# Conditions' and values' bias products moved to the gap in front of the second layer, scale and shift in four operations, bounds of the reciprocals behind the norm

## The chip, the cores and the metric

The kernel runs on one core of a Trainium2 chip. Such a core has a matrix engine (TensorE, PE in the profile; PEld is its weight load, which overlaps), three engines for element-wise work (VectorE or DVE, ScalarE or ACT, GpSimd or POOL) and SyncE (SP), which here does nothing but issue transfers. Each engine takes its instructions in a fixed order from a queue of its own and waits on semaphores for the others. The metric is the time of one execution on the device in microseconds (us); of several executions the median is given.

## The reference

32 sequences of 128 tokens with 512 features go through two layers. `cond` is one vector of 512 for each sequence. Cut to what matters:

```python
# layer 0: attention with 16 heads of 64, then 8 experts that choose their tokens
shift = silu(cond) @ W_ada.T + b_ada
h = ln(x) + shift
q, k, v = split(h @ Wqkv.T);  q, k = ln(q), ln(k)
x = x + softmax(q k^T / sqrt(64)) v @ Wout.T
gate = softmax(tok @ Wgate.T);  vals, idx = top_k(gate.T, 512)
y = gelu(ln(tok[idx]) @ fc1[e].T + b1) @ fc2[e].T + b2
tok = tok.at[idx].add(y * vals)

# layer 1: adaptive norm, attention with 16 heads of 32, adaptive norm, MLP of 2048
def adaln(x, w, b):
    scale, shift = split(cond @ w.T + b)
    return layernorm(x) * (1 + scale) + shift
n = adaln(x, w_adaln1, b_adaln1)
q, k, v = n @ wq.T + bq, n @ wk.T + bk, n @ wv.T + bv
x = x + softmax(q k^T / sqrt(32)) v @ wo.T + bo
h = gelu(adaln(x, w_adaln2, b_adaln2) @ w1.T + b1)
x = x + h @ w2.T + b2
```

Two small products matter for the change. The conditions' product is `cond @ w.T` for both adaptive norms of layer 1: 32 rows by 1024 columns each. The values' bias `bv` is not added to v: since the weights of a softmax add up to one, it can be added behind the attention, as `bv @ wo.T`, to the bias `bo`. That is the values' bias product.

## The kernel before

All work of the fast kernel is first declared as operations: engine, planned duration, buffers that are read and written, a priority number (smaller is earlier) and a job. A list scheduler in the same file (`Sched`) then plans them in time and writes out, for each engine, one fixed order of instructions. Buffers are taken from pools while it plans: 11 weight slots of 1 MB (128 × 4 × 512 float32), 52 row slots of 128 × 512, and 8 banks of PSUM, the matrix engine's accumulators. So a changed priority, or an operation more or less, can change the order of other work and the slots that it takes.

The stages are these:

- **Layer 0** takes two sequences at a time: 16 pairs, whose jobs overlap. Matrix products are cut into quarters and done with seven products in place of eight, with sums of weights made beforehand. `weight_sums` (L1260 to L1274) makes some of these sums on DVE. In the same stage, at low priority, sums of the weights of layer 1 are prepared and stored in memory (the loop over `at_w`, L2067 to L2083).
- **Routing** finds each expert's 512 tokens while PE does the late projections of the last sequences. Then each of the **8 experts** gathers its token rows with indirect transfers (POOL), normalises them, does two products (`u` L1854 and `d` L1918), and adds its output to the rows of `acc` in memory with an indirect transfer that adds (L1950). The last expert does its second product in two halves.
- **Layer 1** takes two sequences at a time: 16 groups. Group 0 can't begin before the last expert's addition has landed in memory. It loads its two sequences (`x2`, L2158), computes mean and variance (L317, L318) and the reciprocal root in steps of DVE on 128 × 2 elements (L299 to L307), normalises (`a_0n`, L2124), transposes on PE (`a_0t`, L1084), and applies scale and shift in the evictions of the transposed tile (`nT`, L2134 on DVE and L2136 on ACT, which read `ss`). The products `qk` (L2193), scores, exponentials and sums follow; `inv` (L1119) is the reciprocal of the softmax's sums, and `oT` (L2312) the normalised output of the heads. Sums of `oT` (`noa`, `nob`, L1108) are operands for the out-projection `o` (L2239); `seven_T` writes the order of its seven products, and of those of `v`. Bias and residual are added to `x3` (L2277 on), whose norm feeds the MLP, `m` (L2359) and `n` (L2420).

What the change touches, as it is before:

- The conditions' products, L1218 to L1240: in the job of the first pair four weight loads of 1 MB (`wad`, L1093) are issued on SP; two times 8 matmuls `pad` (L1229; each is two records of the profile) leave 64 × 512 results, which are copied into one row tile `pads` (ACT L1099 or DVE L1100). In the routing stage four transposes turn them (`ptd`), and 16 operations of DVE (L1238) add the bias, and one for the scale, into `ss1` and `ss2`. `weight_sums` names `pads` among what it reads.
- The values' bias product: in the preparation of `wo`, four copies spread `bv` over 128 columns (`bvb`, L2071), `bo` is loaded (L2073), 8 matmuls `pb` (L2078) take them, DVE adds (L2081), and the result is stored to memory (`bod`, L2015). In layer 1 it is loaded into `bo_t` (L2110).
- The gathers of the experts but the first have a priority 1000 ahead of their expert.
- The two loads of group 0's `x2` are on SP's queue.
- `hi_t` (L2314, POOL) and `lo_t` (L2316, DVE) keep the running sum and the running minimum of the reciprocals; their final values (L2470 to L2478) tell whether the fast kernel's way of taking a softmax without a maximum was safe. Both come directly behind `oT` in priority.

Of the kernel before, what the change touches and what calls it, by code (L numbers as in the profile page):

```python
# [1006 lines left out]
def fast_kernel(ctx: ExitStack, tc: tile.TileContext, x, condT, mask, cols, w_ada, wqkv, wout, wout_p, wout_o, wgate,  # L1007
# [209 lines left out]

    pads, ptd = row("pads"), bank("ptd", (P, 4, P))  # L1218
    RJ = NB // 2
    RP = NB * 100 + 200  # L1220
    for n, (s_, pr, job) in enumerate(((w_adaln1, 140, 1), (w_adaln2, 145, 1))):
        wad = [load_w(s_, 0, j * 512, f"wad_{n}_{j}", 140 + 5 * n, 1, 20.0) for j in range(2)]
        pad = bank(f"pad_{n}")

        def adaln(n=n, wad=wad, pad=pad):
            for k in range(DC):
                for j in range(2):
                    g = 2 * n + j
                    nc.tensor.matmul(pad.t[32 * g : 32 * g + 32, :], cT[:, k, :], wad[j].t[:, k, :],  # L1229
                                     start=(k == 0), stop=(k == DC - 1))  # L1230
        sch.op(PE, mm_us(D, 4), adaln, w=[pad], r=wad, prio=pr, job=job)
        copy([(pads, n)], [pad], lambda n=n: pads.t[64 * n : 64 * n + 64, :], lambda n=n, pad=pad: pad.t[64 * n : 64 * n + 64, :],
             D, pr, job)
    sch.op(PE, 4 * TR, lambda: transpose4(flat(ptd), pads.t), w=[ptd], r=[pads], prio=RP + 900, job=RJ)
    for n, (ss, ssb, nm) in enumerate(((ss1, ss1_b, "b_adaln1"), (ss2, ss2_b, "b_adaln2"))):
        for h in range(2):
            for c in range(4):
                sch.op(DVE, 0.2, lambda ss=ss, nm=nm, n=n, h=h, c=c: nc.vector.tensor_scalar(  # L1238
                    ss[:, 4 * h + c, :], ptd.t[:, c, (2 * n + h) * 32 : (2 * n + h) * 32 + NB], col(nm, 4 * h + c),
                    1.0 - h, ALU.add, ALU.add), w=[(ssb, 4 * h + c)], r=[ptd], prio=RP + 900, job=RJ)  # L1240
# [20 lines left out]
    def weight_sums():  # L1261
        for k in range(2):
            for i, a_, b_, r_ in ((1, lambda k=k: wV(1, 2, k), lambda k=k: wV(1, 1, k), [wqkv_b[4], wqkv_b[5]]),
                                  (2, lambda k=k: wV(2, 2, k), lambda k=k: tv[1][k].t, [wqkv_b[5], tv[1][k]]),
                                  (3, lambda k=k: wV(2, 2, k), lambda k=k: wV(1, 2, k), [wqkv_b[5]]),
                                  (4, lambda k=k: wV(2, 1, k), lambda k=k: tv[2][k].t, [wqkv_b[4], tv[2][k]])):
                o_ = (lambda k=k: wV(1, 2, k)) if i == 3 else (lambda i=i, k=k: tv[i][k].t)
                tt(o_, a_, b_, ALU.subtract, D, [wqkv_b[5] if i == 3 else tv[i][k]], r_ + [pads], 154, 1, DVE, False)
        for n in range(2):
            for i, a_, b_, r_ in ((1, lambda n=n: wB(1, 2, n), lambda n=n: wB(1, 1, n), [wqkv_b[n + 2], wqkv_b[n]]),  # L1270
                                  (2, lambda n=n: wB(2, 2, n), lambda n=n: wT(1, n), [wqkv_b[n + 2], (t12[n], 0)]),
                                  (3, lambda n=n: wB(2, 2, n), lambda n=n: wB(1, 2, n), [wqkv_b[n + 2]]),
                                  (4, lambda n=n: wB(2, 1, n), lambda n=n: wT(2, n), [wqkv_b[n], (t12[n], 1)])):
                tt(lambda i=i, n=n: wT(i, n), a_, b_, ALU.subtract, 2 * D, [wTb(i, n)], r_ + [pads], 155, 1, DVE, False)  # L1274
# [466 lines left out]
    def expert(e, after):  # L1741
# [13 lines left out]
        for h in range(NH):  # L1755
            sch.op(POOL, 1.2, lambda h=h: nc.gpsimd.indirect_dma_start(
                out=xg[h].t, out_offset=None, in_=tok[:, :],
                in_offset=bass.IndirectOffsetOnAxis(ap=idx[:, e, h : h + 1], axis=0)),
                w=[xg[h]], r=[tok_b, (idx_b, e)], lat=2.5, prio=pe_ - 1000 if e else pe_, job=job)
# [255 lines left out]
    bod = dram.tile([P, D], F32, name="bod")  # L2015
    bod_b = stands(bod)
# [10 lines left out]
    sch.op(POOL, 0.5, lambda: nc.gpsimd.memset(lo_b.t, 1.0), w=[lo_b], r=[up_done], prio=LB - 800, job=LJ)  # L2027

# [35 lines left out]
    for m, (n, s_) in enumerate(at_w):  # L2064
        pr, job = 200 * (10 + m) + 195, 10 + m
        q = quarters(s_, f"{n}q_", lambda i, j: (QD * (i - 1), QD * (j - 1)), pr, job)
        if n == "o":  # L2067

            bvb, bos, pb0 = row("bvb", (P, DC, P)), row("bos"), bank("pb0")
            for c in range(DC):  # L2070
                sch.op(DVE, 0.3, lambda c=c: nc.vector.tensor_copy(bvb.t[:, c, :], col("bv", c).to_broadcast([P, P])),  # L2071
                       w=[(bvb, c)], prio=pr - 2, job=job)
            sch.op(SP, 0.06, lambda: nc.sync.dma_start(bos.t, bo.partition_broadcast(P)), w=[bos], lat=4.0, prio=pr - 2, job=job)  # L2073

            def bias0(q=q, bvb=bvb, pb0=pb0):
                for l in (1, 2):
                    for c in range(DC):
                        nc.tensor.matmul(pb0.t[:, (l - 1) * QD : l * QD], bvb.t[:, c, :], q[1 + c // 2, l].t[:, c % 2, :],  # L2078
                                         start=(c == 0), stop=(c == DC - 1))
            sch.op(PE, mm_us(D, DC), bias0, w=[pb0], r=[bvb, *q.values()], prio=pr - 1, job=job)  # L2080
            sch.op(DVE, dve_us(D), lambda: nc.vector.tensor_tensor(bos.t, bos.t, pb0.t, ALU.add), w=[bos], r=[bos, pb0],  # L2081
                   prio=pr - 1, job=job)
            store(bod[:, :], bos, bod_b, None, pr, job)  # L2083
        A = lambda i, j, q=q: q[j, i]
        sa, sb, sc_ = (row(f"{n}s{z}_", (P, 2, QD)) for z in "124")
        for o_, a_, b_, op_ in ((sa, A(2, 1), A(2, 2), ALU.add), (sb, sa, A(1, 1), ALU.subtract),
                                (A(2, 1), A(1, 1), A(2, 1), ALU.subtract), (sc_, A(1, 2), sb, ALU.subtract)):
            tt(lambda o_=o_: o_.t, lambda a_=a_: a_.t, lambda b_=b_: b_.t, op_, D, [o_], [a_, b_], pr, job, DVE, False)
        for z, b_ in enumerate((sa, sb, A(2, 1), sc_)):
            store(s4d[m, z], b_, s4d_b, (m, z + 1), pr, job)  # L2090
# [19 lines left out]
    sch.op(SP, 0.06, lambda: nc.sync.dma_start(bo_b.t, bod[:, :]), w=[bo_b], r=[up_done, bod_b], lat=4.0, prio=LB - 800, job=LJ)  # L2110
# [41 lines left out]
    def group(g):  # L2152
# [4 lines left out]
        for i in range(GB):  # L2157
            sch.op(SP, 0.06, lambda i=i: nc.sync.dma_start(x2[i].t, acc[(b0 + i) * S : (b0 + i + 1) * S, :]),  # L2158
# [70 lines left out]
        def seven_T(n, Bn, rB, Tv, Tn, pr, first, comb, out2):  # L2229
# [16 lines left out]
            out2(1, 1, U[1], ps[2])  # L2246
            prod(6, "s2", lambda: Tv(2), [Tn[2]])
# [10 lines left out]
            prod(3, "s4", lambda: Bn(2, 2), rB(2, 2))  # L2258
# [15 lines left out]
        for i in range(GB):  # L2274
# [27 lines left out]
            def outs(po=po, pe=pe, i=i):  # L2302
                for t in range(4):
# [11 lines left out]
                   w=[hi_b], r=[inv], prio=pa + 20, job=job)  # L2315
            sch.op(DVE, dve_us(D), lambda inv=inv: nc.vector.tensor_tensor(lo_b.t, lo_b.t, flat(inv), ALU.min),  # L2316
                   w=[lo_b], r=[inv], prio=pa + 8, job=job)
# [249 lines left out]
```

## Time and profile before

| | us |
|---|---|
| median of 3 runs | 3264.16 (3264.08 to 3264.27) |
| the profiled execution | 3265.81 |
| its span, first to last instruction | 3264.1 |
| layer 0 | 0 to about 1000 |
| routing, late projections, first gather | about 1000 to 1108 |
| experts | 1108 to 1917.3 |
| gap in front of layer 1 | 1917.3 to 1930.6 |
| layer 1 | 1930.6 to the end |

The span in 40 equal slices; each digit is the busy share of a slice in tenths, and PEclk the clock granted to PE in tenths of full speed. A slice is 81.6 us.

```profile
PE   8999999999999899999999989999999999999999
DVE  7877876787777888666676547666666666666665
ACT  3333332343441122211222213333333333333332
POOL 0011111000023467766676510000000000000000
PEclk9999999999999899999999999999999999999999
```

PE is at nine tenths or more in all slices but three: the first, the routing's, and the one that holds the gap. The profile can miss a few per cent of the matmul records. The clock stands at 0.993 on average.

### The profile page before, as it was taken

Reading aid. Unit: us, or ns where it says so; the run is one execution under the profiler, and the core shown is the slowest. Engines: PE = TensorE matmul, PEld = TensorE weight load, DVE = VectorE, ACT = ScalarE, POOL = GpSimd, SP = SyncE. Lnnn points to the kernel's source line nnn. Section 1 sums busy time; section 2 is a strip of 40 time slices with the busy share of each in tenths; the row PEclk is TensorE's granted clock in tenths of the full one; section 3 lists DMA queues with packets and bytes.
Section 4 is the critical chain, followed back from the end, with each engine's and each line's share of the span. In section 5 each row is a group of like instructions: output and inputs, shape, how many; then the busy total and the mean of one; then the engine's idle time right before and its main releaser. Section 6 shows DMA issues by size and latency. Waiting matters only on the chain.

```text
span 3264.1 us, 55856 instructions
## 1 busy us (share of the span) xinstructions
PE 3204.9 (98%) x21802; PEld 2563.0 (79%) x21802; DVE 2265.9 (69%) x4849; ACT 962.0 (29%) x2307; POOL 709.8 (22%) x561
## 2 busy tenths in 40 slices
PE   8999999999999899999999989999999999999999
PEld 4565566555558688888888878999999999999998
DVE  7877876787777888666676547666666666666665
ACT  3333332343441122211222213333333333333332
POOL 0011111000023467766676510000000000000000
PEclk9999999999999899999999999999999999999999
DMA  5122211321125423433333542333333333333343
GB/s 210 52 66 84 67 55 56 113 82 65 46 91 196 160 86 102 117 110 106 102 110 94 152 142 92 105 101 101 102 100 100 102 98 99 101 100 101 104 136 105
DMA packets 247138, 335.65 MB, mean 103 GB/s; under 512 B 22098, under 2 KB 156498, under 8 KB 246354
## 3 DMA queue, kind: packets, MB, share of 16 engines
q1 hardware_dynamic: 239698, 315.09, 29.4%
q0 software_dynamic: 7168, 16.91, 2.8%
q8 instruction: 174, 2.85, 0.4%
q14 instruction: 98, 0.80, 0.1%
HBM read 277.01 MB, written 54.92 MB: 102 GB/s over the span
## 4 chain that ended last, share of the span: by engine, by line
PE 60%; DVE 2%; issue 1%; ACT 1%; DMA 1%; SPq 0%; DVEq 0%; ACTq 0%
PE m L2359 12%; PE d L1918 12%; PE u L1854 11%; PE n L2420 10%; PE qk L2193 6%; PE v L2239 3%; PE o L2239 2%; PE sc L2289 1%; PE ps L2300 1%; PE po L2306 1%; DVE lo_t L2316 1%; DVE inv L1119 0%; DVE noa L1108 0%; PE tpg L1084 0%; DVE inv_1t L1117 0%
## 5 line engine op out<-in xcount | busy, mean ns | idle before, releaser
L2314 POOL TENSOR_TENSOR hi_t<-hi_t,inv 128x512 f32<-128x512 f32 x32 | 40.8, 1276 | 1229.9 <-DVE inv L1119 1229.9
L2370 ACT ACTIVATE m<-m,prm 128x128 f32<-128x128 f32 x512 | 162.0, 390 | 230.4 <-DVE m L2364 226.3
L1918 PE MATMUL d<-fc,h 128*128 128x256 f32 x992 | 219.0, 380 | 0.6 <-DVE v L1859 0.6
L1918 PEld LDWEIGHTS d<-fc,h 128*128 128x128 f32 x992 | 187.9, 190 | 26.1 <-DVE v L1859 0.8
L1865 ACT ACTIVATE h<-h,prm 128x256 f32<-128x256 f32 x256 | 114.9, 500 | 258.0 <-DVE h L1859 250.6
L1854 PE MATMUL u<-gT,fc 128*128 128x256 f32 x768 | 179.0, 383 | 1.0 <-ACT gT L1824 1.0
L1854 PEld LDWEIGHTS u<-gT,fc 128*128 128x128 f32 x768 | 147.7, 193 | 21.9 <-ACT gT L1824 1.4
L2364 DVE TENSOR_TENSOR m<-mu,m 128x512 f32<-128x512 f32 x128 | 87.9, 687 | 110.2 <-PE m L2359 107.9
L1300 ACT ACTIVATE sq<-qk 128x512 f32<-128x512 f32 x128 | 80.8, 632 | 215.5 <-DVE qk L1338 205.9
L2364 DVE TENSOR_TENSOR mu<-mu,m 128x512 f32<-128x512 f32 x96 | 65.9, 686 | 88.1 <-PE m L2359 88.1
L2359 PE MATMUL m<-n2a,w_s 128*128 128x128 f32 x1024 | 124.8, 275 | 0.0
L2420 PE MATMUL n<-w_t,m 128*128 128x256 f32 x512 | 122.8, 379 | 0.0
L1854 PE MATMUL u<-tg,s 128*128 128x256 f32 x512 | 120.9, 379 | 0.9 <-DVE tg L1108 0.9
L2359 PE MATMUL m<-n2T,w 128*128 128x128 f32 x1024 | 120.0, 275 | 0.2 <-ACT n2T L2136 0.2
L2359 PEld LDWEIGHTS m<-n2a,w_s 128*128 128x128 f32 x1024 | 119.5, 192 | 0.0
L2359 PEld LDWEIGHTS m<-n2T,w 128*128 128x128 f32 x1024 | 118.3, 192 | 1.4 <-ACT n2T L2136 0.4
L1859 DVE TENSOR_TENSOR h<-v,u 128x512 f32<-128x512 f32 x128 | 86.3, 681 | 47.7 <-PE u L1854 46.1
L2420 PE MATMUL n<-w_t,ms 128*128 128x256 f32 x512 | 117.8, 382 | 0.0
L2420 PE MATMUL n<-w,m 128*128 128x256 f32 x512 | 114.7, 382 | 0.0
L1334 PE MATMUL q<-wqkv,hsb 128*128 128x512 f32 x240 | 113.8, 597 | 0.1
L1334 PE MATMUL q<-wqkv,hT 128*128 128x512 f32 x240 | 113.9, 606 | 0.0
L1918 PE MATMUL d<-t,hs 128*128 128x256 f32 x512 | 113.4, 379 | 0.0
(1155 smaller groups left out, 7537.9 us busy)
## 6 DMA issues: line engine op xcount, KB each, us to landing
w_t<-t2d SPq DMA_DIRECT2D x256, 256.0 KB, 3.1
w<-in_w_dram SPq DMA_DIRECT2D x192, 256.0 KB, 4.1
fc<-in_fc_dram SPq DMA_DIRECT2D x64, 512.0 KB, 4.4
fc<-in_fc_dram SPq DMA_DIRECT2D x32, 1024.0 KB, 5.3
x<-in_x_dram SPq DMA_DIRECT2D x32, 256.0 KB, 3.1
xT<-in_xT_dram SPq DMA_DIRECT2D x32, 256.0 KB, 2.7
otd<-oT SPq DMA_DIRECT2D x32, 256.0 KB, 2.1
ol<-otd SPq DMA_DIRECT2D x32, 256.0 KB, 4.1
```

The costliest lines, as they stand in the source:

```text
L1300: sch.op(ACT, act_us(D), lambda: nc.scalar.activation(sq.t, qk[i][j].t, AF.Square), w=[sq], r=[qk[i][j]], prio=pr, job=job)
L1334: nc.tensor.matmul(ps[m].t, lhs()[:, k, :], rhs[0](k), start=(k == 0), stop=(k == 1))
L1854: nc.tensor.matmul(ps[n].t[:, t, :], lhs()[:, k, t * P : (t + 1) * P], rhs.t[:, k, :], start=(k == 0), stop=(k == 1))
L1859: sch.op(DVE, dve_us(D), lambda: nc.vector.tensor_tensor(o_.t, a_.t, ps[n].t, ALU.add), w=[o_], r=[a_, ps[n]], prio=pr, job=job)
L1865: sch.op(ACT, act_us(HQ, 1), lambda t=t, c=c: nc.scalar.activation(o_.t[:, t, :], o_.t[:, t, :], AF.Gelu_apprx_tanh, bias=col("b1s", e * 1 ...
L1918: nc.tensor.matmul(ps[n].t[:, j, :], lhs[m].t[:, k, t * P : (t + 1) * P], rhs.t[:, 2 * m + k, :], start=(m == 0 and k == 0), stop=(m == NM ...
L2193: nc.tensor.matmul(ps[m].t[:, z, u, :], w_()[:, k, u * P : (u + 1) * P], rhs()[:, k, :], start=(k == 0), stop=(k == 1))
L2239: nc.tensor.matmul(ps[m].t, lhs()[:, k, :], w_()[:, k, :], start=(k == 0), stop=(k == 1))
L2359: nc.tensor.matmul(ps[n].t[:, u, :], l1w[what].t[:, k, (NQ * q + u) * P : (NQ * q + u + 1) * P], rhs()[:, k, :], start=(k == 0), stop=(k = ...
L2364: sch.op(DVE, dve_us(D), lambda: nc.vector.tensor_tensor(o_.t, a_.t, ps[n].t, ALU.add), w=[o_, *more], r=[a_, ps[n]], prio=pq_, job=job)
L2370: sch.op(ACT, act_us(S, 1), lambda u=u, c=c: nc.scalar.activation(o_.t[:, u, :], o_.t[:, u, :], AF.Gelu, bias=col("b1", c), scale=1.0), w= ...
L2420: nc.tensor.matmul(ps[n].t, Ah[lhs][c // NQ].t[:, c % NQ, :], b_.t[:, k, :], start=(c == 0), stop=(c == 7))
```

## The change

- The conditions' products with their loads and copies, the transposes, and the scale and shift move to the job of layer 1's group 0. The loads may start when the last expert's first product is done (`up_done`). The priorities put the products at LB − 824 and LB − 823, the transposes and the scale and shift at LB − 822, where LB is the priority from which layer 1 counts.
- Scale and shift are 4 operations of DVE in place of 16: each takes 128 × 4 × 32 elements and a broadcast bias.
- `weight_sums` no longer names `pads`.
- The gathers of the experts from the third on have their own expert's priority.
- The values' bias product moves to group 0's job as well. It takes the out-projection's quarters that layer 1 loads in any case, and a fourth quarter (`wo21`) loaded for it. `bo` is loaded directly into `bo_t`, and DVE adds the product there; the memory tile `bod` and its store and reload are gone.
- Group 0's two loads of `x2` are issued by ACT.
- `seven_T` writes its third product behind the second, in place of last.
- `hi_t` and `lo_t` get priorities behind the work of their group's second norm.

```diff
-    pads, ptd = row("pads"), bank("ptd", (P, 4, P))
...
-    for n, (s_, pr, job) in enumerate(((w_adaln1, 140, 1), (w_adaln2, 145, 1))):
-        wad = [load_w(s_, 0, j * 512, f"wad_{n}_{j}", 140 + 5 * n, 1, 20.0) for j in range(2)]
...
-    sch.op(PE, 4 * TR, lambda: transpose4(flat(ptd), pads.t), w=[ptd], r=[pads], prio=RP + 900, job=RJ)
...
-            for c in range(4):
-                sch.op(DVE, 0.2, lambda ss=ss, nm=nm, n=n, h=h, c=c: nc.vector.tensor_scalar(
-                    ss[:, 4 * h + c, :], ptd.t[:, c, (2 * n + h) * 32 : (2 * n + h) * 32 + NB], col(nm, 4 * h + c),
-                    1.0 - h, ALU.add, ALU.add), w=[(ssb, 4 * h + c)], r=[ptd], prio=RP + 900, job=RJ)
...
-                tt(o_, a_, b_, ALU.subtract, D, [wqkv_b[5] if i == 3 else tv[i][k]], r_ + [pads], 154, 1, DVE, False)
+                tt(o_, a_, b_, ALU.subtract, D, [wqkv_b[5] if i == 3 else tv[i][k]], r_, 154, 1, DVE, False)
...
-                w=[xg[h]], r=[tok_b, (idx_b, e)], lat=2.5, prio=pe_ - 1000 if e else pe_, job=job)
+                w=[xg[h]], r=[tok_b, (idx_b, e)], lat=2.5, prio=pe_ - 1000 if e == 1 else pe_, job=job)
...
+    pads, ptd = row("pads"), bank("ptd", (P, 4, P))
+    for n, (s_, pr, job) in enumerate(((w_adaln1, LB - 824, LJ), (w_adaln2, LB - 823, LJ))):
+        wad = [load_w(s_, 0, j * 512, f"wad_{n}_{j}", LB - 985 + n, LJ, r=[up_done]) for j in range(2)]
+        pad = bank(f"pad_{n}")
+
+        def adaln(n=n, wad=wad, pad=pad):
+            for k in range(DC):
+                for j in range(2):
+                    g = 2 * n + j
+                    nc.tensor.matmul(pad.t[32 * g : 32 * g + 32, :], cT[:, k, :], wad[j].t[:, k, :],
+                                     start=(k == 0), stop=(k == DC - 1))
+        sch.op(PE, mm_us(D, 4), adaln, w=[pad], r=wad, prio=pr, job=job)
...
+    sch.op(PE, 4 * TR, lambda: transpose4(flat(ptd), pads.t), w=[ptd], r=[pads], prio=LB - 822, job=LJ)
+    for n, (ss, ssb, nm) in enumerate(((ss1, ss1_b, "b_adaln1"), (ss2, ss2_b, "b_adaln2"))):
+        for h in range(2):
+            at = COL[nm] + 4 * h
+            sch.op(DVE, 0.3, lambda ss=ss, n=n, h=h, at=at: nc.vector.scalar_tensor_tensor(
+                ss[:, 4 * h : 4 * h + 4, :], ptd.t[:, :, (2 * n + h) * 32 : (2 * n + h) * 32 + NB], 1.0 - h,
+                bcast(prm[:, at : at + 4], NB), ALU.add, ALU.add), w=[(ssb, h)], r=[ptd], prio=LB - 822, job=LJ)
...
-            bvb, bos, pb0 = row("bvb", (P, DC, P)), row("bos"), bank("pb0")
...
-            sch.op(PE, mm_us(D, DC), bias0, w=[pb0], r=[bvb, *q.values()], prio=pr - 1, job=job)
...
-            store(bod[:, :], bos, bod_b, None, pr, job)
...
-    sch.op(SP, 0.06, lambda: nc.sync.dma_start(bo_b.t, bod[:, :]), w=[bo_b], r=[up_done, bod_b], lat=4.0, prio=LB - 800, job=LJ)
+    sch.op(SP, 0.06, lambda: nc.sync.dma_start(bo_b.t, bo.partition_broadcast(P)), w=[bo_b], r=[up_done], lat=4.0, prio=LB - 800, job=LJ)
+
+    bvb, pb0, wo21 = row("bvb", (P, DC, P)), bank("pb0"), row("wo21", (P, 2, QD))
+    for c in range(DC):
+        sch.op(DVE, 0.3, lambda c=c: nc.vector.tensor_copy(bvb.t[:, c, :], col("bv", c).to_broadcast([P, P])),
+               w=[(bvb, c)], r=[up_done], prio=LB - 890, job=LJ)
+    load_at("o21", lambda: wo21.t, wo21, wo[:QD, QD:].rearrange("(k p) n -> p k n", p=P), [up_done], LB - 945, spare=8)
+
+    def bias0():
+        for i in (1, 2):
+            for c in range(DC):
+                nc.tensor.matmul(pb0.t[:, (i - 1) * QD : i * QD], bvb.t[:, c, :], l1w[f"o{i}{1 + c // 2}"][0]()[:, c % 2, :],
+                                 start=(c == 0), stop=(c == DC - 1))
+    sch.op(PE, mm_us(D, DC), bias0, w=[pb0], r=[bvb] + [l1w[f"o{i}{j}"][1] for i in (1, 2) for j in (1, 2)], prio=LB - 821, job=LJ)
+    sch.op(DVE, dve_us(D), lambda: nc.vector.tensor_tensor(bo_b.t, bo_b.t, pb0.t, ALU.add), w=[bo_b], r=[bo_b, pb0],
+           prio=LB - 815, job=LJ)
...
-            sch.op(SP, 0.06, lambda i=i: nc.sync.dma_start(x2[i].t, acc[(b0 + i) * S : (b0 + i + 1) * S, :]),
+            sch.op(*((SP, 0.06) if g else (ACT, 0.1)), lambda i=i: (nc.sync if g else nc.scalar).dma_start(
+                x2[i].t, acc[(b0 + i) * S : (b0 + i + 1) * S, :]),
...
             out2(1, 1, U[1], ps[2])
+            prod(3, "s4", lambda: Bn(2, 2), rB(2, 2))
             prod(6, "s2", lambda: Tv(2), [Tn[2]])
...
-            prod(3, "s4", lambda: Bn(2, 2), rB(2, 2))
             out2(1, 2, U[4], ps[3])
...
-                   w=[hi_b], r=[inv], prio=pa + 20, job=job)
+                   w=[hi_b], r=[inv], prio=pr + 197, job=job)
...
-                   w=[lo_b], r=[inv], prio=pa + 8, job=job)
+                   w=[lo_b], r=[inv], prio=pr + 196, job=job)
```

## The prediction

> **What bounds the kernel now.** I read the busy shares first, then what TensorE waited for, then the busy time by stretches, then the chain of waits and the timeline round the three places that the change touches.
>
> ```profile
> PE 3204.9 (98%) x21802; PEld 2563.0 (79%) x21802; DVE 2265.9 (69%) x4849; ACT 962.0 (29%) x2307; POOL 709.8 (22%) x561
> ```
>
> TensorE (PE) is busy for all but 59 us, so two things can shorten the run: less matmul time in a stretch where PE is full, or less idle PE time. Its waits, largest first (columns: total us, times, longest us):
>
> ```profile
> PE tpg L1084 <- DVE xng L1812: 14.3, 3, 12.8
> PE a_0t L1084 <- DVE a_0n L2124: 13.3, 1, 13.3
> PE tpx L1084 <- DVE xn L1399: 12.6, 3, 10.1
> PE o L2239 <- DVE noa L1108: 4.2, 13, 0.3
> ```
>
> The second is the gap in front of layer 1: the last expert's output is scattered to memory, read back and normalised, with nothing for PE to do. The fourth is a small wait in nearly every group of layer 1. Three stretches follow (stretch, length, busy time of PE, PEld, DVE, ACT, POOL, granted clock, DMA share, GB/s): layer 0, the gap, and the first products behind it.
>
> ```profile
> 600.00:1000.00 400.00, 400.00 (x3006) 226.24 (x3003) 302.57 (x697) 169.13 (x442) 41.45 (x35) 1.00 0.23 78
> 1918.00:1930.00 12.00, 0.00 (x0) 0.00 (x0) 3.54 (x15) 0.00 (x0) 1.55 (x1) 0.68 0.66 174
> 1933.00:1936.00 3.00, 3.00 (x16) 3.00 (x16) 2.24 (x7) 0.97 (x3) 0.00 (x0) 0.50 1.02 406
> ```
>
> Layer 0 has no PE slack (140 to 600 us lacks only 2.4 us); the gap has 12 us of it; and the clock is granted at 0.50 for some 6 us behind the gap.
>
> **Products taken out of layer 0.** The conditions' products (pad, 32 matmul records) and the values' bias products (pb, 16 records) leave layer 0 and the weight preparation. What they hold there:
>
> ```profile
> 104.08 3.63 PE L1229 MATMUL pad<-wad,cT 128*32 128x512 f32 x16
> 107.64 5.42 PE L1334 MATMUL q<-wqkv,hT 128*128 128x512 f32 x12
> ...
> 872.01 3.62 PE L2078 MATMUL pb<-oq,bvb 128*128 128x256 f32 x16
> 875.56 1.07 PE L1473 MATMUL ps<-pe,ones_f 128*32 128x512 f32 x8
> ```
>
> From start to the next start: 107.64 − 104.08 = 3.56 us, and 875.56 − 872.01 = 3.55 us. The first set (78.58 us) has 14 records up to 81.50, 2.92 us, and two more at the same 0.21 = 3.3 us. They were no fillers: when the first set ran, the exponentials for the sums behind it had ended 4.6 us before (73.98 us). Sum: 3.3 + 3.6 + 3.5 = **−10.4 us**, if PE stays as full as the row 600:1000 has it.
>
> The schedule of layer 0 is drawn anew, though: in the instruction order of the changed kernel the first sequences' work, up to about sequence 30, is shuffled by several places, and one transposing step now waits for a sum made just ahead of it. For a wait of that kind the trace has the small ones of its list, 0.2 to 1.4 us each; I take +0.5, bounds −2.5 (the two tpx waits beside the 10.1, 12.6 − 10.1, gone) to +4 (three new ones). With the products go two copies to an SBUF row, four copies that spread bv, an addition, a store and its reload, and from SP's queue four 1 MB loads at 0.37 us an issue: none was on PE's path (DVE 302 of 400 us busy, ACT 169), 0. The routing's four transposes (0.64 us at 1095.00) and 16 scale and shift operations (2.63 us at 1095.67) ran while PE waited for the gathered rows, the first of which started at 1099.33 us behind the token stores: worth 0. Expert gathers moved behind other work on POOL are issued one or two operations later, and PE has no idle time in 1180 to 1870 us (690 of 690): 0.
>
> **The gap.** Before, in order:
>
> ```profile
> 1916.74 0.59 PE L1918 MATMUL d<-fc,hs 128*128 128x256 f32 x2
> 1917.38 0.48 DVE L1943 SCALAR_TENSOR_TENSOR y<-d,gsel,w 128x256 f32<-128x256 f32 x1 [2.97 <-PE d L1918]
> 1918.14 1.55 POOL L1950 DMA_INDIRECT acc<-y,idx  x1 [5.35 <-DVE y L1943]
> 1923.18 2.71 SPq L2158 DMA_DIRECT2D x<-acc  x6
> 1925.86 0.69 DVE L317 BATCH_NORM_STATS2 a_0st<-x 128x6 f32<-128x512 f32 x1 [8.00 <-DMA x<-acc]
> ...
> 1928.25 0.16 DVE L303 SCALAR_TENSOR_TENSOR a_0t<-a_0y 128x2 f32<-128x2 f32 x1
> ...
> 1930.61 1.97 PE L1084 MATMUL a_0t<-ident,a_0n 128*128 128x128 f32 x8 [13.27 <-DVE a_0n L2124]
> 1932.37 1.99 PE L2193 MATMUL qk<-nT,wq 128*128 128x128 f32 x8
> ```
>
> The changed order puts on PE, directly behind the last product d (end 1917.33): pad_0, pad_1, pb, four transposes (ptd). By the durations above, 3.6 + 3.6 + 3.6 + 0.64 = 11.4 us, so ptd ends at about 1928.8. On DVE the four new scale and shift operations stand *ahead* of the nine small steps of the norm's root, and wait for ptd. The nearest row for one (128x128, the same kind, 1941.64 us) is 0.30: 4 × 0.30 = 1.2 us. They start at 1928.85 and end at 1930.05, and the step that started at 1928.25 starts there: **+1.8 us** for a_0t and all behind it. Its bounds: group 0's two loads of x are issued by ACT now, for which the trace has no row; the nearest are SP's 0.33 to 0.47 and POOL's 0.95 to 1.56 us an issue. At SP's price the loads land as before. At POOL's they land 1.2 us later, of which 0.6 are hidden behind ptd: +2.4. On ACT's queue the second pad's copy stands behind these issues, which wait for the scatter (1923.18); it is needed at about 1924.7, and ptd at 1928.1, so this is free, with 3 us to spare. If the matmuls run as densely as the first pad set's 0.21 us a record (32 × 0.21 + 3.55 + 0.64 = 10.9, ptd at 1928.2), it is the four operations and the wait for their input alone: +1.3, the bound below.
>
> The loads must be there: the conditions' four take slots whose former users' loads were issued at 1855 to 1872 us, the out-projection's weights come last, into slots freed by the last expert's second half near 1907 us, and a 256 KB piece landed in 3.2 to 6.5 us here: 1916 at the latest, needed at 1924.5. Cover: 8 us.
>
> The clock: PE's idle stretch shrinks from 13.3 to 3.6 us. The row against a gain: an idle stretch of 3.1 us, 1152 to 1155.1, was also followed by a clock of 0.50 for 6 us. So I take 0 for the cold start; if the clock stays up, the 5.4 us at half rate give back up to 1.3 (the first products also wait for evictions, at 0.8 us a pair): bounds −1.3 to 0. [...]
>
> **Bounds of the reciprocals behind the norm.** The wait at o, in a steady group:
>
> ```profile
> 2114.10 0.69 DVE L2312 TENSOR_TENSOR oT<-po,inv 128x512 f32<-128x512 f32 x1
> 2114.21 1.27 POOL L2314 TENSOR_TENSOR hi_t<-hi_t,inv 128x512 f32<-128x512 f32 x1 [4.20 <-DVE inv L1119]
> 2114.71 1.32 DVE L2316 TENSOR_TENSOR lo_t<-lo_t,inv 128x512 f32<-128x512 f32 x1
> ...
> 2115.95 0.41 DVE L1108 TENSOR_TENSOR noa<-oT,oT 128x256 f32<-128x256 f32 x1
> 2116.39 0.42 DVE L1108 TENSOR_TENSOR noa<-oT,noa 128x256 f32<-128x256 f32 x1
> ```
>
> lo_t, 1.3 us, stands between oT and noa; PE then waits 0.32 us at 2116.64. lo_t now comes six operations later. hi_t on POOL keeps its place (nothing else is there), and ends at 2115.48. If noa could not start before that, it would still end at 2116.3, 0.3 ahead of PE. So the wait goes: 13 × 0.32 = **−4.2 us**, bounds −4.2 and 0. What is late next is x and its norm, by one lo_t; PE's wait for that norm's result is 0.2 us in the whole run.
>
> [...]
>
> The third product moved to third place (v and o) changes nothing that is counted: the same 16 records, PE full.
>
> **Sum.** −10.4 + 0.5 + 1.8 − 4.2 = −12.3 us. On the profiled execution, span 3264.1 (3265.81 with its surroundings), that is 3251.8; the median of the runs, 3264.16, lies beside the span, so **3251.9 us**. Its own range: all bounds good, −10.4 − 2.5 + 1.3 − 1.3 − 4.2 = −17.1, 3247; all bad but for the o wait, −10.4 + 4 + 2.4 − 4.2 = −8.2, 3256; with that wait left too, −4.0, 3260.
>
> **Rivals.**
>
> *The gap is full of a new wait* (0.13). If the out-projection's load were held until the last d had ended (1917.3) and took 11.2 us, as a 1 MB load there did, pb would start at 1928.5 and ptd, in order behind it, end at 1932.8; with the four operations the norm would go on at 1934.0 instead of 1928.25: +5.8 in place of +1.8. 3255.9. Against it: the second half's first operands are given back 10 us earlier.
>
> *Layer 0 gives nothing back* (0.10). The shuffled order spends the 10.4 us in new small waits; left are +1.8 − 4.2: 3261.8, no change. For it: the scheduler places by planned costs, and the order differs up to sequence 30. Against it: 2.4 us idle in 460.
>
> *Slower by a wait in each pair* (0.08). In the new order the normalised rows of the next pair (xn, then tpx) come later in the queue of DVE. The list has such waits at 12.6 us in three, two of them 1.25 us; one of 1.4 in each of 16 pairs is +22, and the sum 3273.9. It turns slower than before at 12.3 / 16 = 0.77 us a pair. Against it: order and waits from sequence 30 on are as before, so at most 14 pairs could show it.
>
> *The change doesn't do what it says* (0.01): that the products aren't in the gap. The order has them directly behind the last d.
>
> **How the numbers follow.** Forecast 0.68. A measurement here tells 0.2%, 6.5 us, from no change: faster is below 3257.6, slower above 3270.7. Faster: 0.68 and 0.13, nearly whole, less a tail: 0.79. Same: 0.10 and 0.03 of tails, 0.13. Slower: 0.08. The range, 3247 to 3259, holds the forecast's bounds but for the last us of the bad end, and the first rival; it leaves out the second and third, 0.18.
>
> **What would show it.** PE busy time in 0 to 1000 us less by some 10 us and its idle time as before, and the gathers' stage starting that much earlier: right on layer 0. pad, pb and ptd back to back, a_0t's wait 3 to 4 us, and the four operations ahead of the norm's steps: right on the gap. A wait of pb for a load: the first rival. "PE o <- noa" gone from the list and lo_t at 0.69 where hi_t has ended: right on the bounds. New waits at tpx or q over 5 us in all would make the prediction wrong, and so would a clock of 1.00 behind the gap, by one us to the good.

## The result and the profile after

The changed kernel takes 3253.71 us (median of 7 runs, 3253.49 to 3257.01) beside 3265.16 us of the kernel before (7 runs, 3264.08 to 3266.08). The ratio is 0.9968, with a 95% interval of 0.9957 to 0.998: faster by some 0.3%. The span of the profiled execution went from 3264.1 to 3253.6 us, by 10.5; the forecast was 12.3. The page of the changed kernel:

```profile
span 3253.6 us, 55850 instructions
...
PE 3203.5 (98%) x21802; PEld 2561.4 (79%) x21802; DVE 2259.1 (69%) x4850; ACT 957.6 (29%) x2292; POOL 716.3 (22%) x563
```

Its waits of PE (total us, times, longest us):

```profile
PE tpg L1084 <- DVE xng L1790: 13.3, 3, 12.1
PE tpx L1084 <- DVE xn L1377: 11.1, 2, 9.9
PE a_0t L1084 <- DVE a_0n L2121: 5.3, 1, 5.3
PE u L1832 <- DVE v L1837: 4.2, 1, 4.2
PE m L2357 <- ACT n2T L2133: 1.4, 1, 1.4
```

The wait of o for noa is gone, and the wait in the gap fell from 13.3 to 5.3 us because 9.5 us of products stand in it now. Of the lines shown two are longer than before: u's wait for v (3.1 to 4.2) and m's for n2T (0.2 to 1.4). Two that the list before did not have follow them: tpg waits 1.2 us for h in front of the first d, and tpq 0.9 us for qk in layer 0. The time between landmarks of the two profiles says where the 10.5 us lie:

| stretch, us | before | after | difference | forecast |
|---|---|---|---|---|
| start to the first gather (POOL) | 1099.33 | 1090.50 | −8.8 | −9.9 |
| first gather to the first product d | 77.6 | 78.5 | +0.9 | 0 |
| first d to the last y | 740.4 | 741.5 | +1.1 | 0 |
| last y to a_0t (the gap) | 13.2 | 14.7 | +1.4 | +1.8 |
| a_0t to the end (layer 1) | 1333.5 | 1328.4 | −5.1 | −4.2 |

The gap, in the timeline of the changed kernel:

```profile
1906.87 3.62 PE L1896 MATMUL d<-fc,hs 128*128 128x256 f32 x16
1910.41 5.38 PE L2014 MATMUL pad<-wad,cT 128*32 128x512 f32 x32
1910.52 0.48 DVE L1921 SCALAR_TENSOR_TENSOR y<-d,gsel,w 128x256 f32<-128x256 f32 x1 [2.97 <-PE d L1896]
...
1915.73 3.72 PE L2103 MATMUL pb<-wo,bvb 128*128 128x256 f32 x16
1916.01 0.84 ACTq L2155 DMA_DIRECT2D x<-acc  x2
1916.04 1.79 SPq L2155 DMA_DIRECT2D x<-acc  x4
...
1919.28 0.60 PE L1084 MATMUL ptd<-ident,pads 128*128 128x128 f32 x4
1919.70 0.69 DVE L317 BATCH_NORM_STATS2 a_0st<-x 128x6 f32<-128x512 f32 x1 [8.69 <-DMA x<-acc]
...
1922.05 0.88 DVE L2023 SCALAR_TENSOR_TENSOR ss<-ptd,prm 128x128 f32<-128x128 f32 x4
...
1925.19 1.97 PE L1084 MATMUL a_0t<-ident,a_0n 128*128 128x128 f32 x8 [5.31 <-DVE a_0n L2121]
```

The products stand back to back behind the last d, and nothing waits for a load. But the gap grew by another way than forecast. The 32 records of pad took 5.3 us and not 7.2, so ptd was done at 1919.9, before DVE had finished the statistics: the four operations did not wait for it. Their own 0.88 us stand in front of the norm's steps, and x came late: from issue to the first statistics 3.7 us (1916.01 to 1919.70) where it was 2.7 before (1923.18 to 1925.86).

### The profile page after: what moved, and what is told of

Read it like the earlier page. It is cut to its first block, busy times and chain, and to the rows that moved or that the text cites. A ratio compares the mean times of both kernels' runs of the same rounds, so it can differ in the third digit from the quotient of the medians.

```text
span 3253.6 us, 55850 instructions
## 1 busy us (share of the span) xinstructions
PE 3203.5 (98%) x21802; PEld 2561.4 (79%) x21802; DVE 2259.1 (69%) x4850; ACT 957.6 (29%) x2292; POOL 716.3 (22%) x563
```

## The experiments

Kernels that begin with b_ are the kernel before with one part of the change, those with a_ the changed kernel with one thing altered (a_gap and a_warm each add one to the run before). A profile's landmarks are shown where the time alone is too coarse: the 95% intervals of the ratios are ±0.09 to ±0.14%, 3 to 4.5 us.

### The bounds alone, and the third product alone

b_bounds has only the new priorities of hi_t and lo_t:

```diff
-                   w=[hi_b], r=[inv], prio=pa + 20, job=job)
+                   w=[hi_b], r=[inv], prio=pr + 197, job=job)
-                   w=[lo_b], r=[inv], prio=pa + 8, job=job)
+                   w=[lo_b], r=[inv], prio=pr + 196, job=job)
```

> The kernel before with the new priorities of hi_t and lo_t alone. Theory: this is what layer 1 gained (from its first transposes to the end 1333.5 us before, 1328.4 after, 5.1 less); layer 1 shortens by 4.2 to 5.1, the 13 waits of o for noa (4.2 us) are gone, the time is 3259 to 3260 beside 3264. Rival: the third product's earlier place gave layer 1 its gain; then layer 1 stays within 1 us of 1333.5 and the time is 3263 to 3265.

b_third has only the moved product:

```diff
             out2(1, 1, U[1], ps[2])
+            prod(3, "s4", lambda: Bn(2, 2), rB(2, 2))
...
-            prod(3, "s4", lambda: Bn(2, 2), rB(2, 2))
             out2(1, 2, U[4], ps[3])
```

> The kernel before with the third of the seven products written behind the second, and nothing else. Theory: nothing, PE does the same records in a full stretch: layer 1 1333.5 within 0.5, the waits of o for noa stay at about 4. Rival: it gives the 0.9 us of layer 1's gain that the bounds' 4.2 leave open, or removes the waits of o itself by putting a product in front of those that need noa.

b_bounds: 3261.64 us, ratio 0.9987 (0.9978 to 0.9996), span 3258.6. Layer 1 fell from 1333.5 to 1329.2 us, by 4.3, and o waits for noa but once, for 0.2 us: the whole −4.2 of the forecast comes with the new priorities. The time, 3.9 us under the 3265.53 of the kernel before in the same runs, is a little short of the 4 to 5 that were expected. (The span fell by 1.2 more ahead of layer 1, where this kernel's instructions are those of the kernel before.) b_third: 3267.31 us, ratio 1.0006 (0.9997 to 1.0015), which alone can't be told from no change. Layer 1 is 1335.3 us, 1.8 *longer*; the waits of o stay at 4.2. Both theories of the third product were wrong: alone it neither gives nothing nor gains. The loss lies in the first three groups (a_3t comes 174.4 us behind the first transposes, 172.6 before), where the first groups' work is put in another order and the transposes of group 0's second norm wait, which they did not before; the wait is 1.05 of the 1.8:

```profile
1983.83 1.06 PE L1084 MATMUL a_0t<-ident,a_0n 128*128 128x128 f32 x8 [1.05 <-DVE a_0n L2124]
```

In the steady groups it changes nothing by itself (82.8 us from group to group, as before). The changed kernel has b_third's order there, operation for operation, but for one lo_t a group, which stands six operations later (compared in groups 6 and 9), and takes 82.4 us: lo_t's place alone is worth 0.4 us a group. b_bounds takes 82.5. Layer 1's 5.1 in place of 4.3, against b_bounds, is 0.9 lost in the first three groups (172.6 beside 171.7), 1.2 gained over the next twelve (989.0 beside 990.2) and 0.5 behind them. How much of that is the third product is not shown: PE's order differs between these two in other products too, and no run has the bounds and the third product alone.

### The conditions alone, the bias product alone, and length without order

b_cond moves the conditions' products, b_bias the bias product, each with the diff's own lines and nothing else.

> The kernel before with the conditions' products, the four scale and shift operations and their loads moved to the gap; no other part. Theory: layer 0 shortens by the 6.9 us that the two sets held, so the last transposes of the gate's products start near 999.5 (1006.4 before); of that the first gather keeps at most what the late projections allow, and the time falls by 4 to 6, to 3258 to 3260. Rival: layer 0's gain comes of the new order and not of the products' length; then the last transposes lie anywhere between 996 and 1006 and not near 999.5.

> The kernel before with the values' bias product moved to the gap; no other part. Theory: the gate's last transposes start 3.5 us earlier, near 1002.9, the gap keeps its length within 0.5 since pb (3.6 us) lies inside its 13.3 us, and the time is 3261 to 3262. Rival: pb or the added load delays the gap's norm, or the later bias in the residual makes layer 1 wait: the gap grows by 1 us or more and the time is 3263 or above.

b_short keeps the order of the kernel before and leaves records out:

```diff
-            for k in range(DC):
+            for k in range(1):
...
-                    for c in range(DC):
+                    for c in range(1):
...
```

> The kernel before in its own order, instruction for instruction, with three quarters of the conditions' products (24 of 32 records) and of the bias product (12 of 16) left out; scale, shift and bias are then wrong. It takes the length out of layer 0 without any shuffle. Theory: each record gives back its pitch, 24 x 0.222 = 5.3 us in layer 0's first 110 us and 12 x 0.222 = 2.7 us near 872 us, 8.0 us at the last gate's products, all of it kept up to the gathers. Rival: the neighbours take part of it back (the changed kernels kept 7 to 9 of 10.4, the bias product alone 2.5 of 3.5), because what stands behind the products has work of other engines to wait for or records that ran beside them: then 5 to 6.5 us here, in the same order.

b_cond: 3261.77 us, ratio 0.9986 (0.9977 to 0.9995). b_bias: 3263.75 us, 0.9994 (0.9985 to 1.0003). b_short: 3261.18 us (3254.70 to 3267.63), 0.9987 (0.9978 to 0.9997). In time b_cond gave 3.8 us and b_bias 1.8, a little less than expected (4 to 6, and 2 to 3).

At the gate's last transposes b_cond is 6.7 us ahead of the order before and b_bias 3.1, near the 6.9 and 3.5 of the theory. But that is partly luck. In both, and in the changed kernel, the new order has moved 8 records of the projections' product w (1.7 us) from ahead of these transposes to behind them: 384 records follow up to the last, 376 in the order before. So the lead is read where PE has the same records behind it, those of pad, pb and the transposes ptd aside. What the profiles differ in at 60.7 us already, where PE has done the same in all (it gets there at 59.4 to 61.1 us), is taken off. The table has the lead over the kernel before in us (with a minus, the run is behind); the changed kernel, a_ptd, a_gap and a_warm have one order up to layer 1, and so have b_bounds, b_third and the kernel before:

| | 112 us, behind both sets of conditions | 749 us | 966 us, behind the bias product | 1095 us, last product before the gathers | first gather |
|---|---|---|---|---|---|
| order before (2 more profiles) | 0.2 | 0.1 to 0.2 | 0.1 to 0.2 | 0.2 | 0.1 to 0.2 |
| changed order (4 profiles) | 6.5 | 5.8 | 9.3 | 7.4 to 7.9 | 8.6 to 9.3 |
| b_cond | 6.7 | 6.0 | 6.1 | 4.7 | 6.2 |
| b_bias | 0.2 | 0.2 | 2.6 | −0.9 | 1.2 |
| b_short | 5.1 | 5.3 | 6.4 | 5.8 | 5.8 |

Three things can be read off. First, the conditions gave nearly their whole length where they stood: 6.7 and 6.5 us of 6.9, and 5.1 of the 5.3 that b_short left out of an untouched order, 2.6 for each set. The bias product gave 3.4 of 3.5 in the changed order (from 749 to 966 us it gains 3.5, b_cond 0.1). So up to there it is the products' length and not a lucky order. In b_short the bias product gave only 1.1 of 2.7, since PE meets a wait for DVE:

```profile
873.32 1.98 PE L1334 MATMUL q<-wqkv,hT 128*128 128x512 f32 x4 [0.91 <-DVE bos L2081]
```

That wait is for the addition of the bias product itself, which b_short keeps and which the change takes away with the product. The rival of the last expectation held in number (5 to 6.5 us; 5.8 are left), but by this wait and 0.6 us lost behind 1016 us; the conditions gave theirs in full.

Second, each new order loses between 966 us and the last product: 1.4 to 1.9 us in the changed one, 1.3 in b_cond, 3.5 in b_bias, where 0.6 of it are the transposes ptd, which stand there now. In the changed kernel 1.3 of 1.9 is idle time of PE by 991 us, most of it one wait of the kind that the prediction had named:

```profile
970.65 1.56 PE L1084 MATMUL tpq<-ident,qk 128*128 128x128 f32 x12 [0.91 <-DVE qk L1403]
```

Third, the new orders get part of it back at the gathers, which follow the last product after 3.6 to 3.7 us in the changed order, 5.0 before. The last products, additions, token stores and the first gather, before and then in the changed kernel:

```profile
1092.46 1.89 PE L1545 MATMUL w<-wout,os 128*128 128x256 f32 x8
1094.01 1.11 DVE L1561 TENSOR_TENSOR xl<-w,xl 128x256 f32<-128x256 f32 x3 [0.62 <-POOL xl L1109]
1095.68 0.40 SPq L1567 DMA_DIRECT2D tok<-xl  x1
1099.33 1.16 POOL L1756 DMA_INDIRECT xg<-tok,idx  x1 [4.67 <-issue]
```

```profile
1084.88 1.89 PE L1523 MATMUL w<-wout,os 128*128 128x256 f32 x8
1086.88 0.42 DVE L1539 TENSOR_TENSOR xl<-w,xl 128x256 f32<-128x256 f32 x1 [1.37 <-PE w L1523]
1087.33 0.32 SPq L1545 DMA_DIRECT2D tok<-xl  x1
1090.50 1.16 POOL L1734 DMA_INDIRECT xg<-tok,idx  x1 [5.62 <-issue]
```

Before, DVE's last additions waited for POOL's; now they wait for PE alone, and the last token store is issued 0.6 us behind the last product in place of 1.3.

### The gap: order, queue, clock

a_ptd lets the bias product read the transposes, so that they come first:

```diff
-    sch.op(PE, mm_us(D, DC), bias0, w=[pb0], r=[bvb] + [l1w...
+    sch.op(PE, mm_us(D, DC), bias0, w=[pb0], r=[bvb, ptd] + [l1w...
```

> The changed kernel with the bias product made to wait for the conditions' transposes, so that PE's order in the gap is pad, ptd, pb and the four scale and shift operations stand ahead of the first statistics on DVE; nothing else. Theory: the four operations (0.88 us) inside the chain of the norm are one of two things that lengthen the gap. ptd follows the second copy (near 1917.5), the four end near 1919.2, before x has landed (1919.7): from the last product d to the first transposes 15.1 us become 14.2, and the time falls by 0.9. Rival: the operations cost nothing since DVE waits for something else; the gap stays 15.1.

a_gap has this and the two loads on SP:

```diff
-            sch.op(*((SP, 0.06) if g else (ACT, 0.1)), lambda i=i: (nc.sync if g else nc.scalar).dma_start(
+            sch.op(SP, 0.06, lambda i=i: nc.sync.dma_start(
```

> The same, and group 0's two loads of x issued on SP again. Theory: the loads on ACT start beside the four of the next groups on SP and share the transfer engines with them, so that the first lands in 3.7 us in place of 2.7; in one queue the first two land first: the gap loses another 0.8 us, to 13.3 to 13.5 us as before the change, and the time is 1.7 below the changed kernel. Rival: ACT's issue makes no difference to the landing; the gap is as in the kernel with the order alone.

a_warm has both and:

```diff
+    pw0 = bank("pw0")
+
+    def fill():
+        for c in range(DC):
+            nc.tensor.matmul(pw0.t[:, :QD], bvb.t[:, c, :], l1w[f"o1{1 + c // 2}"][0]()[:, c % 2, :],
+                             start=(c == 0), stop=(c == DC - 1))
+    sch.op(PE, mm_us(QD, DC), fill, w=[pw0], r=[pb0, bvb] + ..., prio=LB - 820, job=LJ)
```

> The same as the kernel with both mended, and 4 matmuls more (8 records, 1.8 us) behind pb, into a bank that nothing reads. They add nothing to the result. Theory: PE's idle stretch falls from about 3 us to about 1, the clock is granted at 1.00 behind the gap in place of 0.50 for 4 us, and layer 1 from its first transposes is shorter by 1 to 2 us. Rival: the first products wait for the evictions of the transposed tile anyway, so the clock changes nothing beyond 0.3 us; or the added matmuls run into the transposes and cost up to their 1.8 us.

a_ptd: 3254.21 us, ratio 0.9965 (0.9952 to 0.9979). a_gap: 3252.05 us, 0.9958 (0.9944 to 0.9971). a_warm: 3250.1 us, 0.9955 (0.9941 to 0.9968). These intervals overlap, and a_ptd's median is not below the changed kernel's 3253.71, so the gap itself decides: from the start of y to a_0t 13.2 us before, 14.7 in the changed kernel, 14.0 in a_ptd and 12.8 in a_gap. The order is worth 0.7: the first statistics start 9.2 us behind y in the changed kernel and in a_ptd, but the first reciprocal-root step on a_0t at 11.6 in place of 12.3. The queue is worth 1.2: in a_gap the first statistics start at 8.3. Neither part alone lengthens the gap: b_cond, whose loads are on SP and whose four operations end before x has landed, has 13.2 us, and b_bias 13.0, as was expected of it. Profiles whose gap is the old one scatter from 12.6 to 13.2. The timeline of a_gap:

```profile
1912.28 1.55 POOL L1928 DMA_INDIRECT acc<-y,idx  x1 [5.35 <-DVE y L1921]
...
1916.99 2.72 SPq L2155 DMA_DIRECT2D x<-acc  x6
1917.50 0.66 PE L1084 MATMUL ptd<-ident,pads 128*128 128x128 f32 x4 [0.71 <-ACT pads L1099]
1917.99 3.62 PE L2103 MATMUL pb<-wo,bvb 128*128 128x256 f32 x16
1918.19 0.88 DVE L2023 SCALAR_TENSOR_TENSOR ss<-ptd,prm 128x128 f32<-128x128 f32 x4 [6.19 <-PE ptd L1084]
1919.80 0.69 DVE L317 BATCH_NORM_STATS2 a_0st<-x 128x6 f32<-128x512 f32 x1 [0.73 <-DMA x<-acc]
```

The four operations end at 1919.1, while DVE has nothing else to do, and x lands 2.8 us after its issue. For the clock, the stretches behind the gap (stretch, length, busy PE, PEld, DVE, ACT, POOL, granted clock, DMA share, GB/s), first of a_gap, where PE had stood idle for 2.7 us:

```profile
1926.00:1928.00 2.00, 2.00 (x11) 2.00 (x11) 1.04 (x3) 1.20 (x3) 0.00 (x0) 0.50 0.99 393
1928.00:1930.00 2.00, 2.00 (x18) 2.00 (x17) 1.97 (x6) 0.89 (x3) 0.00 (x0) 0.85 1.06 440
```

and of a_warm, where 1.8 us of matmuls for nothing left 1.1 us idle:

```profile
1924.00:1926.00 2.00, 2.00 (x21) 2.00 (x20) 1.44 (x5) 1.34 (x4) 0.00 (x0) 1.00 1.05 434
1926.00:1928.00 2.00, 2.00 (x20) 2.00 (x19) 2.00 (x5) 0.00 (x0) 0.00 (x0) 1.00 1.03 422
```

PE does 20 records in 2 us in place of 11. Layer 1 is 1327.0 us in place of 1327.9: the slow clock behind the gap costs 0.9 us there, just short of the 1 to 2 that were expected. In the changed kernel, where the transposes a_0t ran at the slow clock as well (0.50; 1.97 us beside 1.22 in a_gap), layer 1 is 1328.4 us, 1.4 more than in a_warm.

### The first expert: GpSimd holds VectorE out

In the changed kernel's first expert, on POOL, DVE and PE:

```profile
1129.74 4.93 POOL L1109 TENSOR_TENSOR t<-fc,fc 128x512 f32<-128x512 f32 x4
1134.64 4.93 POOL L1109 TENSOR_TENSOR t<-fc,t 128x512 f32<-128x512 f32 x4
1139.55 4.92 POOL L1109 TENSOR_TENSOR fc<-fc,fc 128x512 f32<-128x512 f32 x4
...
1130.14 14.88 DVE L1108 TENSOR_TENSOR hs<-h,h 128x512 f32<-128x512 f32 x1
...
1146.43 0.89 PE L1832 MATMUL u<-tg,fc 128*128 128x256 f32 x3 [4.18 <-DVE v L1837]
```

One operation of DVE, 0.68 us where it is shortest, takes 14.88 us: it ends at 1145.02 us, 0.55 us behind a row of twelve POOL operations of 1.23 us each (1144.47). a_pool2 puts half of the twelve on DVE:

```diff
-                   ALU.subtract, D, [(o_, h)], [(a_, h), (b_, h)] + ([] if e else [y]), pe_ - 600 + 1000 + n, job, POOL, False)
+                   ALU.subtract, D, [(o_, h)], [(a_, h), (b_, h)] + ([] if e else [y]), pe_ - 600 + 1000 + n, job, DVE if e == 0 and h % 2 else POOL, False)
```

> The changed kernel with half of the twelve weight sums of the first expert's second product (t1, t2, fc2, one operation of 128x512 each) put on DVE in place of POOL. Theory: DVE's operation of 14.9 us in the first expert is DVE kept out by twelve POOL operations in a row; PE's wait of 4.2 us for it, the waits of 1.2 and 0.7 and the slow clock behind them are where 1.9 us of layer 0's gain went. With the row broken up the long operation is gone, no DVE operation there is over 2 us, and the time from the first gathered transposes to the first d (69.4 us) falls to 64 to 67: 3 to 5 us in all. Rival: DVE is simply full there (it does six more operations now, 4.1 us); the waits stay in sum as long, the time is the same or longer.

a_pool2: 3247.64 us, ratio 0.9946 (0.9932 to 0.9959). From the first gathered transposes to the first d it takes 62.7 us in place of 69.4, and the wait of u for v is gone. Not as expected: an operation of over 2 us is still there, the first of these two with 6.46.

```profile
1133.74 7.06 DVE L1108 TENSOR_TENSOR t<-fc,t 128x512 f32<-128x512 f32 x2
```

### All that helped, together

best6 is a_warm with a_pool2's edit; best12 is the same with all twelve sums on DVE (`POOL if e else DVE`).

> The changed kernel with the three things that helped: the conditions' transposes ahead of the bias product, group 0's loads on SP with four matmuls more behind the bias product (into a bank that nothing reads), and half of the first expert's twelve weight sums on DVE. Theory: the gains add, as they lie in different stretches: 6.6 (weight sums) and 1.9 (gap) and 0.9 (clock behind the gap) below the changed kernel, a span near 3243 and a time of 3243 to 3246. Rival: the earlier end of the experts meets loads that are not there yet; the gap grows again and 2 us or more are lost.

> The same with all twelve weight sums of the first expert on DVE. Theory: what costs is POOL holding DVE out, 7.1 us of it are left with six sums; with none on POOL no DVE operation of the first expert is longer than 2 us, and the time from the first gathered transposes to the first d falls below the 62.7 us of the kernel with six, by 1 to 3 us. Rival: DVE is full by then (six operations more at 0.65 us, 3.9 us) and the time is the same or up to 2 us longer than with six.

best6: 3243.51 us, ratio to the kernel before 0.9934 (0.992 to 0.9947); the gains add. best12: 3250.41 us, 0.9954 (0.994 to 0.9967): from the first gathered transposes to the first d 67.6 us, 4.9 more than with six. DVE's longest operations there are two of 2.2 and 2.4 us, a little over the 2 us of its theory, and yet its rival held, by more than its 2 us: the twelve take DVE 10.7 us between 1128 and 1141 us, ahead of its own work, and PE waits 5.5 us for the normalised rows of the next expert, 2.2 in best6. Beside a_warm (3250.1 us), from which it differs in the sums alone, best12 gains nothing, where half of the sums gave best6 6.6.

## Why the prediction was right, and where it was not

The forecast was −12.3 us and the span fell by 10.5. Part of the nearness is luck, as errors offset each other: layer 0 gave 1.1 less than forecast and the experts lost 2.0 that were not in the sum, while the gap came out 0.4 and layer 1 0.9 better.

**Layer 0, −10.4 + 0.5.** The mechanism held, and so did "They were no fillers": the products gave 9.9 of their 10.4 us where they stood (6.5 and 3.4). Mis-sized is the +0.5 for the new order. It took 0.7 us by 749 us and 1.4 to 1.9 between 966 us and the last product, and gave back 1.3 at the gathers, which the sum did not have. In all, the gathers start 8.6 to 9.3 us earlier in place of 9.9: with the 0.5 us that the products themselves fell short, +1.1 to +1.8 in place of +0.5, inside its bounds. PE's idle time from 70 us to the last product grew by only 0.5 us (3.9 before, 4.5 after), so "if PE stays as full" held for the idle time. Part of the rest is that the same records take longer in another order: behind 1041 us 0.5 us more, without idle time. What makes that is open.

**Gathers and routing, 0.** Right for the gathers: b_cond, with the old priority, has the same time from the first gather to the first d (78.5 us in both). The 0.9 and 1.1 us that the experts gave back were not forecast, and their cause is not settled. All five profiles with the conditions in layer 0 (the kernel before, b_bounds, b_third, b_bias, b_short) have 77.6 us to the first d and 740.4 from there to the last y. Of the five with the conditions moved and the experts as they were (b_cond and the four of the changed order) only a_warm has the same; the others lie at 77.9 to 78.5 and 741.5 to 743.5. u's longer wait is not it: b_bounds has it at 4.2 us too, with 77.6. What the slower ones share is a clock of 0.50 to 0.71 in the 4 us behind the first d, where the others have 1.00; as a_warm has the changed order too, the order alone doesn't decide it (below).

**The gap, +1.8; measured +1.4.** Right in size, but partly by luck. The four operations cost 0.7 (1.2 forecast, at 0.30 each; they took 0.22). The other half of the forecast, their wait for ptd, did not arise, as the end of the first set of pad and the start of the second ran side by side (four records in 0.43 us, two elsewhere), 0.17 us a record over all 32 in place of 0.22. In its place stand the loads, 1.2, of which the upper bound had kept 0.6 for a dearer issue. The issue on ACT was not dear (0.42 us each; SP's four beside them took 0.45 each); what cost was that the six loads no longer went in one queue. The two halves are counted from a_gap's 12.8, which is 0.4 under the kernel before. The first rival's late loads did not occur.

**The clock, 0.** Right: after 5.3 us idle the clock was 0.50 (1926 to 1928 us), as it was before after 13.3 us idle (1933 to 1936 us), and the upper price of 1.3 us is near what a_warm measured: 0.9 beside a_gap, 1.4 beside the changed kernel.

**The bounds, −4.2; measured −4.3.** Right with its working. The timeline of a steady group:

```profile
2108.81 1.27 POOL L2312 TENSOR_TENSOR hi_t<-hi_t,inv 128x512 f32<-128x512 f32 x1 [4.19 <-DVE inv L1119]
2109.48 0.88 DVE L1108 TENSOR_TENSOR noa<-oT,oT 128x256 f32<-128x256 f32 x1
...
2110.39 0.43 DVE L1108 TENSOR_TENSOR noa<-oT,noa 128x256 f32<-128x256 f32 x1
...
2111.08 1.03 PE L2237 MATMUL o<-wos,noa 128*128 128x256 f32 x4
...
2112.19 0.68 DVE L2314 TENSOR_TENSOR lo_t<-lo_t,inv 128x512 f32<-128x512 f32 x1
```

noa runs beside hi_t now, as lo_t did before: it takes 0.88 in place of 0.41 us and ends 0.3 us behind hi_t (2110.1). The second noa is done 0.3 us ahead of PE, as worked out. The lo_t that moved, apart from hi_t, takes 0.68 in place of 1.32 (0.69, oT's length, was the author's estimate); the other of the group, beside hi_t, still takes 1.27.

**The third product, "changes nothing".** Wrong for the first three groups: +1.8 us alone. Right for the steady ones, alone. What it does together with the bounds is not shown.

**The rivals.** That layer 0 gives nothing did not come true: 8.6 to 9.3 of 10.4 us reached the gathers. The slower one, a wait in each pair, did not occur: the waits of tpx fell from 12.6 to 11.1 us. The change did what it said.

## What to carry to other kernels

A product taken out of a full stretch of one engine, with the operations that need it, gave nearly its whole length where it stood (9.9 of 10.4 us); what the new order takes or gives behind it is a term of its own. Read the gain where the same work lies behind the engine: a landmark that the order moves showed a gain of 1.7 us that was none. Work put into a gap is free only off the gap's own chain: its last operations belong ahead of what the chain waits for (0.7 us in a_ptd), and the chain's loads in front of the others in one queue (1.2 us in a_gap). Where a DVE operation is many times as long as its like (14.88 us beside 0.68), look at what ran on POOL until its end.

## What the runs showed of the hardware that was not expected

In the first expert one DVE operation (`hs<-h,h`, 128x512) began in a row of twelve POOL operations without a pause and did not end before the last of them: 14.88 us in the changed kernel, its end 0.55 us behind theirs. It was in the kernel before as well (14.86 us, again 0.55 us behind). With half of the twelve on DVE (a_pool2) one DVE operation of 6.46 us was left, with all twelve there (best12) none of the first expert was over 2.4 us. It was worth more than half of the change's gain: 6.1 us by a_pool2's median.

The granted clock fell behind short waits too, and not each time. a_ptd and a_warm have the same order up to the gap, and in front of the first d the same waits of 0.7 and 0.6 us; in the 4 us behind, the clock was 0.61 in a_ptd and 1.00 in a_warm:

```profile
1169.00:1173.00 4.00, 4.00 (x13) 3.27 (x12) 3.93 (x9) 2.16 (x5) 3.64 (x3) 0.61 0.04 14
```

```profile
1168.00:1172.00 4.00, 4.00 (x19) 3.51 (x19) 3.93 (x9) 2.16 (x5) 3.86 (x4) 1.00 0.14 48
```

PE does 13 records of d in one and 19 in the other. In the four profiles of this order it takes 740.0 to 743.1 us from the first d to the last (740.0 to 740.1 in the three of the order before). That is as much as most of the parts studied here, and a reason to compare stretches and not only times.
